# Fixed first tiles for eight experts, small last groups in a linear attention, and an order for norms and scatters

## The chip, the cores and the metric

The program runs on one NeuronCore of a Trainium2 chip, in float32 throughout. The metric is the device time of one execution in microseconds (us). Five engines work side by side, each through its own instructions in order: TensorE (PE, matmuls; PEld are its weight loads), VectorE (DVE), ScalarE (ACT), GpSimd (POOL) and SyncE (SP, which here only issues DMAs and reads registers). A DMA is issued by SP, ACT or POOL and carried out by 16 DMA engines. Engines wait for each other through semaphores.

## The reference

Two layers work on x of shape (2, 256, 56, 56). Layer 0 is a group norm, a 1x1 and a depthwise 3x3 convolution to q, k, v, and two neighbourhood attentions (7x7, dilations 1 and 2). Layer 1 turns the image into 6272 tokens of 256 channels and applies a linear attention block and then a mixture of experts:

```python
t = _to_tokens(x)
t = t + _L1_attn_ref(_ln_t(t), ...)   # elu+1 linear attention, layer norm, 512-wide MLP, layer norm
t = t + _L1_ffn_ref(_ln_t(t), ...)    # 8 experts, top 2 of a softmax
x = _from_tokens(t, x)
```

In the experts, each token goes through the two experts that its router likes best, and the results are weighted and added:

```python
h = gelu(einsum('end,edh->enh', xe, W1) + b1)      # 256 -> 1024, per expert
y = einsum('enh,ehd->end', h, W2) + b2             # 1024 -> 256
out = (weights[:, :, None] * sel).sum(axis=1)      # the two chosen experts
```

## The kernel before, in words

The tile framework (`tc`) inserts all semaphores. It also chooses the order of instructions on every engine: it plays the program through with its own clock and issues what is ready, earlier source lines first among ready ones; `tc.high_priority()` puts a block ahead of other ready work, and `tc.issue_after` holds a block behind one instruction. Only TensorE's order in the linear attention is written out by hand (`tc.manual_schedule`). The order is fixed when the program is built; the chip then runs each queue in that order.

**Front.** Convolutions and neighbourhood attention write tokens to `td` in HBM. Behind the last of these stores (`anchors["tokens"]`, L805), SP copies NDUM = 7 blocks of 256 filler rows (`c_fill`, 260 KB each) into the spare region of `xs` (L807). `check_sums` (L811) and then `layer1` (L1070) follow; `layer1` first loads the tokens of the second image, `t_b`, on SP (L1078, L197).

**Linear attention.** The 6272 tokens are 49 blocks of 128. `groups` are six groups of 4 blocks (0 to 23), block 24, and six groups of 4 (25 to 48); written (first block, number of blocks). `order` (L1414) runs them with block 24 last. A software pipeline over steps s (L1421) has five generators in flight: `queries` for order[s], `message` for order[s-1], `feed_forward` for order[s-2], `route` for order[s-3], and the rest of `route` ("p") for order[s-4]. The string in L1434 says in which sequence their parts are traced, and that is TensorE's order:

```python
for part in "mqfpufmuqfurfvrfvfv":
    next(on.get(part, iter(())), None)
```

`feed_forward` has one part for each of four 128-wide hidden blocks (matmuls `p`, L1279) and one part for each two blocks of its second matmul (`py`, L1291), after which a norm's power (POOL, L222), a scaling (DVE `u`, L1300) and an addition to `t_b` (POOL, L1304) follow. `route` starts with `stats` on that sum (DVE L214, L215, L221; POOL power L222), a second power (L1353), and the normalised row (L137), which TensorE transposes (`pts`, L1151). Its second part computes router logits (`pl`, L1371) and the top two (L1307 to L1340). Its third part ranks tokens within their experts (`pp`, L1386 and L1387), turns ranks into row numbers `si` (L1395), and POOL scatters the rows to `xs` in HBM (L143), two indirect DMAs a block. Expert e owns rows from e * RG on, in order of arrival; `cnt` counts them.

**Experts.** When `cnt` is final, a matmul and some twenty small DVE operations make tables (L1473 to L1519): how many 256-row tiles each expert has, and for each of NTL = 56 tiles its expert (`tab[:, 0]`, one-hot `oh`) and first row (`tab[:, 1]`). SP reads eight registers and copies 256 filler rows behind the last row of each expert (L1527). Then for each tile, SP reads expert and row from the table and `fetch` (L1533) loads the rows `xr`, 1 MB `w1e`, 1 MB `w2e` and the bias `b2e`; TensorE transposes (`px`, L1570), multiplies (`ph`, L1581, `py`, L1589); ACT does the gelu (L1585), POOL scatters results to `y` (L1599). At the end, `y` is read back, added and transposed out (L1603).

Of the kernel before, what the change touches and what calls it, by code (L numbers as in the profile page):

```python
# [11 lines left out]
F32 = mybir.dt.float32  # L12
AF = mybir.ActivationFunctionType
ALU = mybir.AluOpType
AX = mybir.AxisListType
# [3 lines left out]
P = 128  # L19
# [20 lines left out]
E = 8  # L40
FF = 1024
NJ = FF // P
N = B * T
K = 2
ST = 256
RG = T * B + ST
NTL = (N * K + E * (ST - 1)) // ST
NDUM = NTL - N * K // ST
XW = C + 4


def shape_constants():
# [24 lines left out]
    def key_masks(n, nk):  # L77
# [18 lines left out]
        "c_steps": np.tile(ST * np.arange(N // ST + 1, dtype=np.float32), (P, 1)),  # L96
        "c_cum": np.tile((np.arange(E)[:, None] >= np.arange(E)[None]).astype(np.float32), (P, 1, 1)),
        "c_tile": np.tile(np.arange(NTL, dtype=np.float32), (P, 1)),
# [10 lines left out]
def hybrid_kernel(ctx: ExitStack, tc: tile.TileContext, a: dict, out: bass.AP):  # L109
# [98 lines left out]
    def stats(sm, t):  # L208

        n = t.shape[1]  # L210
        st = sm.tile([P, 4, 6], F32, name="st")
        mv = sm.tile([P, 4, 2], F32, name="mv")
        for k in range(n):
            nc.vector.bn_stats(st[:, k, :], t[:, k, :])  # L214
            nc.vector.bn_aggr(mv[:, k, :], st[:, k, :])  # L215
        return mv, rstd(sm, mv[:, :n, 1], 1.0)
# [112 lines left out]
    def front(ph):  # L329
# [474 lines left out]
        with tc.issue_after(anchors["tokens"]):  # L804
            for i in range(NDUM):  # L805
                nc.sync.dma_start(xs[E * RG + i * ST : E * RG + (i + 1) * ST, :], a["c_fill"][E + i])
# [263 lines left out]
    def layer1(ctx, tk):  # L1070
# [5 lines left out]
        groups = [(4 * i, 4) for i in range(6)] + [(24, 1)] + [(25 + 4 * i, 4) for i in range(6)]  # L1076
        for n0, n in groups[7:]:
            tk.load(n0, n)  # L1078

        with ExitStack() as ph:  # L1080
# [8 lines left out]
            def load(name, src, shape):  # L1089
                w = wp.tile(shape, F32, name=name)  # L1090
                nc.gpsimd.dma_start(w, src)
                return w
# [63 lines left out]
            def parts(n0, n):  # L1156

                if n == 4:
                    return [(n0 // 25, 0, 4 * P)]
                return [(0, 0, P // 2), (1, P // 2, P)]  # L1160
# [181 lines left out]
            def route(n0, n):  # L1342
# [3 lines left out]
                mv, rs = stats(sm, t)  # L1346
                rs = rs[:, :n]
                u = sm.tile([P, 4], F32, name="u4")[:, :n]
                nc.vector.tensor_tensor(u, mv[:, :n, 1], rs, ALU.mult)
                nc.vector.tensor_tensor(u, u, rs, ALU.mult)  # L1350
                nc.vector.tensor_scalar(u, u, 1e-5, None, ALU.add)
                rs2 = sm.tile([P, 4], F32, name="rs2")[:, :n]
                nc.gpsimd.tensor_tensor(rs2, u, mhalf[:, :n], ALU.pow)  # L1353
# [60 lines left out]
            order = groups[:6] + groups[7:] + groups[6:7]  # L1414
# [4 lines left out]
            with tc.manual_schedule(engines={mybir.EngineType.PE}):  # L1419
                on = {}  # L1420
                for s in range(ng + 4):  # L1421
                    on = {"p": on.get("r", iter(()))}
                    if s < ng:
                        on["q"] = queries(*order[s], qzs)
                    if 1 <= s < ng + 1:
                        on["m"] = message(*order[s - 1], qzs.pop(0), m2Ts)
                    if 2 <= s < ng + 2:
                        on["f"] = feed_forward(*order[s - 2], m2Ts.pop(0))
                    if 3 <= s < ng + 3:
                        on["r"] = route(*order[s - 3])  # L1430
                    if s < 6:
                        for k in range(2):
                            on["uv"[k]] = keys(tk, wk, sm, ps_a, 4, kx, acc, groups[7 + s][0] + 2 * k, 2)
                    for part in "mqfpufmuqfurfvrfvfv":  # L1434
                        next(on.get(part, iter(())), None)
                    if s == 5:
                        kxs = wk.tile([P, 2, C], F32, name="kxs", tag="u")
                        kc = sm.tile([P, 2], F32, name="kc")
                        close_keys(tk, ps_a, kx, acc, kxs, kc)
                        sums[1] = merged(1, kxs, kc)  # L1440
# [3 lines left out]
        with ExitStack() as ph:  # L1444
            wp = ph.enter_context(tc.tile_pool(name="p4w", bufs=1))
            w1p = ph.enter_context(tc.tile_pool(name="p4w1", bufs=3))
            w2p = ph.enter_context(tc.tile_pool(name="p4w2", bufs=3))
# [6 lines left out]
            def load(name, src, shape):  # L1454
# [10 lines left out]
            steps = load("steps", a["c_steps"], [P, N // ST + 1])  # L1465
            cum = load("cum", a["c_cum"], [P, E, E])
            tnum = load("tnum", a["c_tile"], [P, NTL])
            enum = load("enum", a["c_e"], [P, E])
            ones = wp.tile([P, P], F32, name="ones4")
            nc.vector.memset(ones, 1.0)  # L1470


            pc = ps_t.tile([P, E], F32, name="pc", tag="pt")  # L1473
            nc.tensor.matmul(pc, ones, cnt, start=True, stop=True)
            ce = wp.tile([P, E], F32, name="ce")
            nc.vector.tensor_copy(ce, pc)

            endf = wp.tile([P, E], F32, name="endf")
            nc.vector.tensor_tensor(endf, ce, ebase, ALU.add)
            endi = wp.tile([P, E], mybir.dt.int32, name="endi")  # L1480
            nc.vector.tensor_copy(endi, endf)

            ns = N // ST + 1
            gt = wp.tile([P, E, ns], F32, name="gt")
            nc.vector.tensor_tensor(
                gt, ce.unsqueeze(2).to_broadcast([P, E, ns]),
                steps.unsqueeze(1).to_broadcast([P, E, ns]), ALU.is_gt,
            )
            nt = wp.tile([P, E], F32, name="nt")
            nc.vector.tensor_reduce(nt, gt, AX.X, ALU.add)  # L1490
            nc.vector.tensor_tensor(cum, cum, nt.unsqueeze(1).to_broadcast([P, E, E]), ALU.mult)
            incl = wp.tile([P, E], F32, name="incl")
            nc.vector.tensor_reduce(incl, cum, AX.X, ALU.add)

            ge = wp.tile([P, NTL, E], F32, name="ge")
            nc.vector.tensor_tensor(
                ge, tnum.unsqueeze(2).to_broadcast([P, NTL, E]),
                incl.unsqueeze(1).to_broadcast([P, NTL, E]), ALU.is_ge,
            )
            et = wp.tile([P, NTL], F32, name="et")  # L1500
            nc.vector.tensor_reduce(et, ge, AX.X, ALU.add)
            nc.vector.tensor_scalar(et, et, float(E - 1), None, ALU.min)
            etm = wp.tile([P, NTL], F32, name="etm")
            nc.vector.tensor_scalar(etm, et, -float(E), None, ALU.add)
            tab = wp.tile([P, 2, NTL], mybir.dt.int32, name="tab")
            nc.vector.tensor_copy(tab[:, 0, :], et)
            skip = wp.tile([P, E], F32, name="skip")
            nc.vector.tensor_scalar(skip, nt, -float(ST), float(RG), ALU.mult, ALU.add)
            nc.vector.tensor_tensor(ge, ge, skip.unsqueeze(1).to_broadcast([P, NTL, E]), ALU.mult)
            rt = wp.tile([P, NTL], F32, name=f"rt{run}")  # L1510
            nc.vector.tensor_reduce(rt, ge, AX.X, ALU.add)
            nc.vector.scalar_tensor_tensor(rt, tnum, float(ST), rt, ALU.mult, ALU.add)
            nc.vector.tensor_scalar(rt, rt, float(E * RG + (NDUM - 1) * ST), None, ALU.min)
            nc.vector.tensor_copy(tab[:, 1, :], rt)
            oh = wp.tile([P, NTL, E], F32, name="oh")
            nc.vector.tensor_tensor(
                oh, et.unsqueeze(2).to_broadcast([P, NTL, E]),
                enum.unsqueeze(1).to_broadcast([P, NTL, E]), ALU.is_equal,
            )  # L1519

# [6 lines left out]
            for e in range(E):  # L1527
                r = value(endi[0:1, e : e + 1], E * RG - ST)
                ins = nc.sync.dma_start(xs[bass.ds(r, ST), :], a["c_fill"][e])
                tc.declare_no_dep(ins.ins, group=f"xs{run}", reason="rows of their own")  # L1530
                tc.add_to_no_dep_group(f"xs{run}", ins.ins)

            def fetch(t):  # L1533
                e = value(tab[0:1, 0, t : t + 1], E - 1)
                r = value(tab[0:1, 1, t : t + 1], E * RG + (NDUM - 1) * ST)
                xr = xp.tile([P, 2, XW], F32, name="xr")
                nc.sync.dma_start(xr, xs[bass.ds(r, ST), :].rearrange("(p j) c -> p j c", j=2))
# [13 lines left out]

            for t in range(NTL):
                xr, w1e, w2e, b2e = fetch(t)

                eq = xp.tile([P, 2], F32, name="eq")
                nc.vector.tensor_scalar(eq, xr[:, :, C + 3], etm[:, t : t + 1], None, ALU.is_equal)
# [4 lines left out]
                so = xp.tile([P, 4 + NJ, E], F32, name="so")  # L1561
                nc.gpsimd.tensor_tensor(  # L1562
                    so, sel, oh[:, t, :].unsqueeze(1).to_broadcast([P, 4 + NJ, E]), ALU.mult
                )
                sv = xp.tile([P, 4 + NJ], F32, name="sv")
                nc.vector.tensor_reduce(sv, so, AX.X, ALU.add)  # L1566
# [112 lines left out]
```

## Time and profile before

| | |
|---|---|
| median of six runs | 2289.43 us (2281.72 to 2294.22) |
| profiled execution, its own time | 2296.86 us |
| span of its trace | 2295.1 us |
| busy: PE / PEld / DVE / ACT / POOL | 2047.4 / 1434.9 / 1037.4 / 630.1 / 670.2 us |
| front | 0 to about 809 us |
| linear attention, first `t_b` load to last scatter | about 820 to 1373 us |
| tables and filler rows, up to the first expert matmul | about 1373 to 1392 us |
| experts | about 1392 to 2215 us |
| read back and output | about 2216 to 2295 us |

The span is cut out of one execution by the hardware profiler; its times are microseconds from the first instruction. A line of the time-ordered view gives start, duration, engine, source line, operation, written tile and read tiles, how many were merged, and in brackets how long the engine had been idle and what ended that. A line of the table by stretches gives the length of the stretch, each engine's busy time with its number of instructions, TensorE's granted clock as a share of full speed, and what the DMA engines did.

### The profile page before, as it was taken

To read this page: it belongs to the slowest core of one execution; us is meant where nothing else is said; L and a number is where in the kernel's file an instruction comes from. 1 tells how busy PE (TensorE), PEld (TensorE's weight loads), DVE (VectorE), ACT (ScalarE), POOL (GpSimd) and SP (SyncE) were. 2 spreads that over 40 slices of the span, in tenths; PEclk is the share of its full clock that TensorE was granted. 3 is DMA by queue.
4 is the path that set the end of the run, shared out by engine and by line. 5 is a ranking of instruction groups with operands and counts; after the bars stand their busy time and mean duration, and the time that the engine had idled before them with its cause. 6 is when DMAs were issued, how large, how long until landed. Compare 5 with 4: busy or idle time off the path is not lost.

```text
span 2295.1 us, 28356 instructions
## 1 busy us (share of the span) xinstructions
PE 2047.4 (89%) x10344; PEld 1434.9 (63%) x10344; DVE 1037.4 (45%) x2499; ACT 630.1 (27%) x1253; POOL 670.2 (29%) x838
## 2 busy tenths in 40 slices
PE   6899899999988868999999937999999999999963
PEld 3444344554355545666566626888888888888852
DVE  6769867957965543565545441111111111111113
ACT  1223333233332313332333202222222222222210
POOL 5621101120033233453444551222222222222233
PEclk9999889999898979999999968999999999999975
DMA  4643313351522040000001027555555555555537
GB/s 96 155 110 106 95 56 103 97 146 39 159 65 48 26 157 1 1 29 28 26 31 38 33 61 273 187 187 191 192 192 187 187 188 187 190 191 192 170 116 236
DMA packets 175393, 273.79 MB, mean 119 GB/s; under 512 B 24246, under 2 KB 123012, under 8 KB 175006
## 3 DMA queue, kind: packets, MB, share of 16 engines
q1 hardware_dynamic: 155726, 229.99, 32.8%
q0 software_dynamic: 11680, 32.05, 4.1%
q10 hardware_dynamic: 7840, 9.86, 1.2%
q8 instruction: 84, 1.38, 0.3%
q14 instruction: 63, 0.52, 0.1%
HBM read 210.54 MB, written 65.31 MB: 120 GB/s over the span
## 4 chain that ended last, share of the span: by engine, by line
PE 65%; DVE 15%; POOL 5%; DMA 4%; ACT 3%; issue 3%; SPq 1%; DVEq 0%; POOLq 0%; ACTq 0%
PE ph L1581 17%; PE py L1589 17%; PE p L1279 5%; PE po L540 4%; PE py L475 4%; PE pc L487 4%; DVE yc L500 3%; PE s_ps L527 2%; DVE p L531 2%; PE kp L253 2%; DMA yr<-y 2%; POOL rs L222 2%; PE s_ps L325 2%; PE kx L266 2%; PE py L1291 1%
## 5 line engine op out<-in xcount | busy, mean ns | idle before, releaser
L1581 PE MATMUL ph<-xe,w1e 128*128 128x256 f32 x1792 | 401.2, 382 | 13.9 <-DVE xe L1573 10.6
L1589 PE MATMUL py<-w2e,hT 128*128 128x256 f32 x1792 | 395.9, 379 | 0.0
L1581 PEld LDWEIGHTS ph<-xe,w1e 128*128 128x128 f32 x1792 | 339.7, 191 | 66.3 <-DVE xe L1573 17.2
L1585 ACT ACTIVATE hT<-ph,sv 128x256 f32<-128x256 f32 x448 | 209.6, 474 | 598.8 <-PE ph L1581 598.2
L1589 PEld LDWEIGHTS py<-w2e,hT 128*128 128x128 f32 x1792 | 340.5, 190 | 46.3
L500 DVE SCALAR_TENSOR_TENSOR yc<-ypad,w,yc 128x1120 f32<-128x1120 f32 x192 | 267.7, 1397 | 41.2 <-ACT yc L498 38.2
L1594 DVE TENSOR_TENSOR yt<-py,b2e 128x512 f32<-128x512 f32 x56 | 38.8, 692 | 331.8 <-PE py L1589 331.8
L487 PE MATMUL pc<-ypad,diag 128*128 128x448 f32 x432 | 176.6, 549 | 0.5 <-ACT ypad L481 0.5
L531 DVE TENSOR_TENSOR p<-s_ps,tab 98x340 f32<-98x340 f32 (+5 forms) x240 | 138.1, 600 | 62.8 <-PE s_ps L527 61.0
L475 PE MATMUL py<-x_sb,wq 128*128 128x448 f32 (+1 forms) x384 | 156.3, 539 | 10.1 <-ACT yc L491 4.7
L1596 POOL TENSOR_SCALAR yt<-yt,eq 128x256 f32<-128x256 f32 x112 | 52.4, 477 | 366.5 <-DVE yt L1594 366.5
L536 ACT ACTIVATE p<-p 98x680 f32<-98x680 f32 (+5 forms) x120 | 111.8, 931 | 173.7 <-DVE p L531 168.6
L527 PE MATMUL s_ps<-qT,kT 32*98 32x170 f32 (+5 forms) x960 | 132.0, 407 | 18.7 <-DVE p L531 16.7
L1558 DVE TENSOR_TENSOR idi<-xr,eq 128x2 int32<-128x2 f32 x56 | 9.0, 161 | 288.0 <-DMA y<-yt,idi 287.9
L527 PEld LDWEIGHTS s_ps<-qT,kT 32*98 32x98 f32 (+1 forms) x960 | 58.4, 172 | 106.7 <-DVE p L531 60.0
L487 PEld LDWEIGHTS pc<-ypad,diag 128*128 128x128 f32 x432 | 78.1, 189 | 71.7 <-issue 67.6
L143 POOL DMA_INDIRECT y<-yt,idi x112 | 113.1, 1010 | 27.5 <-issue 18.4
L464 POOL TENSOR_SCALAR diag<-ident,w 128x128 f32<-128x128 f32 x108 | 84.1, 800 | 118.6 <-PE pc L487 112.0
L475 PEld LDWEIGHTS py<-x_sb,wq 128*128 128x128 f32 x384 | 70.7, 197 | 73.2 <-issue 54.7
L143 POOL DMA_INDIRECT xs<-row,si x98 | 95.9, 978 | 59.0 <-DVE si L1395 31.7
L1562 POOL TENSOR_TENSOR so<-sel,oh 128x96 f32<-128x96 f32 x56 | 21.5, 388 | 260.6 <-DVE sv L1566 257.8
L222 POOL TENSOR_TENSOR rs<-rs,mhalf 128x2 f32<-128x2 f32 (+2 forms) x88 | 64.9, 744 | 107.8 <-DVE rs L221 101.4
(280 smaller groups left out, 2719.4 us busy)
## 6 DMA issues: line engine op xcount, KB each, us to landing
w1e<-in_L_ffn_W SPq DMA_DIRECT2D x56, 1024.0 KB
w2e<-in_L_ffn_W SPq DMA_DIRECT2D x56, 1024.0 KB
yd<-yc SPq DMA_DIRECT2D x24, 784.0 KB
xr<-xs SPq DMA_DIRECT2D x56, 260.0 KB
ld<-yd SPq DMA_DIRECT2D x28, 448.0 KB
yr<-y SPq DMA_DIRECT2D x12, 1024.0 KB
b2e<-in_L_ffn_b SPq DMA_DIRECT2D x56, 128.0 KB
out<-o_sb ACTq DMA_DIRECT2D x24, 256.0 KB
```

Source lines behind the costliest of these rows:

```text
L143: ins = nc.gpsimd.indirect_dma_start(out=dst[:, :], out_offset=bass.IndirectOffsetOnAxis(ap=index, axis=0), in_=src, in_offset=None,)
L222: nc.gpsimd.tensor_tensor(r[:, :n], r[:, :n], mhalf[:, :n], ALU.pow)
L475: nc.tensor.matmul(py[:, :n, :], wq1[:, ct, oc * P : (oc + 1) * P], x_sb[:, ct, (q0 + g0) * WW : (q0 + g0 + n) * WW], start=(ct == 0), sto ...
L487: nc.tensor.matmul(pc, diag[:, tap, :], ypad[:, dy : dy + 8, dx : dx + WW], start=(tap == 0), stop=(tap == 8),)
L500: nc.vector.scalar_tensor_tensor(yc[:, 8:, :], src, w, yc[:, 8:, :], ALU.mult, ALU.add)
L527: nc.tensor.matmul(s_ps[:nk, j, :n].rearrange("p (i j) -> p i j", j=nj), kT[hs], q[hs], start=True, stop=True,)
L531: nc.vector.tensor_tensor(p[:nk, 2 * pr : 2 * pr + 2, :n].rearrange("p h (i j) -> p h i j", j=nj), s_ps[:nk, :, :n].rearrange("p h (i j) - ...
L536: nc.scalar.activation(p[:nk, :, :n], p[:nk, :, :n], AF.Exp)
L1279: nc.tensor.matmul(p1[:, :w], fw1[:, k, oc * P : (oc + 1) * P], rhs, start=(k == 0), stop=(k == 3))
L1581: nc.tensor.matmul(p1, w1e[:, ct, j * P : (j + 1) * P], xe[:, ct, :], start=(ct == 0), stop=(ct == 1),)
L1585: nc.scalar.activation(hT[:, j, :], p1, AF.Gelu, bias=sv[:, 4 + j : 5 + j])
L1589: nc.tensor.matmul(py[:, h, :], hT[:, j, h * P : (h + 1) * P], w2e[:, j, :], start=(j == 0), stop=(j == NJ - 1),)
```

## The change

1. **Order and size of the last groups.** The last group of four (45, 4) becomes (45, 2) and (47, 2), and block 24 comes before them. The list is now defined ahead of its use and has 14 entries instead of 13, and steps with no new queries use another string.
2. **Route's norms.** `stats`, the second power and what lies between them get high priority.
3. **First tiles.** Tile e < 8 is always expert e's first 256 rows: expert, row and bias selection are known when the program is built. Rows of `xs` that this tile may read but nobody writes are filled by eight more copies beside the seven in the front. The tables (now for 48 tiles) and the eight copies of filler rows, now starting no earlier than row 256 of an expert, are traced after tiles 0 and 1; the first eight `xr` loads and those copies are declared to be independent of each other.
4. **Weights' memory.** The pools of constants, `w1e` and `w2e` wait for the old tiles that they overlap instead of for whole old pools.

```diff
+            for e in range(E):
+                nc.sync.dma_start(xs[e * RG : e * RG + ST, :], a["c_fill"][e])
             for i in range(NDUM):
...
+        order = groups[:6] + groups[7:12] + [(24, 1), (45, 2), (47, 2)]
...
-                if n == 4:
-                    return [(n0 // 25, 0, 4 * P)]
+                if n > 1:
+                    return [(n0 // 25, 0, n * P)]
...
-                mv, rs = stats(sm, t)
...
-                nc.gpsimd.tensor_tensor(rs2, u, mhalf[:, :n], ALU.pow)
+                with tc.high_priority():
+                    mv, rs = stats(sm, t)
...
+                    nc.gpsimd.tensor_tensor(rs2, u, mhalf[:, :n], ALU.pow)
...
-            order = groups[:6] + groups[7:] + groups[6:7]
...
-                    for part in "mqfpufmuqfurfvrfvfv":
+                    for part in "mqfpufmuqfurfvrfvfv" if s < ng else "mfpffmfrfrff":
...
-            w1p = ph.enter_context(tc.tile_pool(name="p4w1", bufs=3))
+            w1p = ph.enter_context(tc.tile_pool(name="p4w1", bufs=3, reuse_waits="tile"))
...
+            def make_tables():
...
+                nc.vector.tensor_scalar(endf, ce, float(ST), None, ALU.max)
+                nc.vector.tensor_tensor(endf, endf, ebase, ALU.add)
...
+                    for group in (f"xs{run}", f"first{run}"):
+                        tc.declare_no_dep(ins.ins, group=group, reason="rows of their own")
+                    tc.add_to_no_dep_group(f"fill{run}", ins.ins)
...
             def fetch(t):
-                e = value(tab[0:1, 0, t : t + 1], E - 1)
-                r = value(tab[0:1, 1, t : t + 1], E * RG + (NDUM - 1) * ST)
                 xr = xp.tile([P, 2, XW], F32, name="xr")
+                if t < E:
+                    e, r = t, t * RG
+                else:
+                    e = value(tables.tab[0:1, 0, t - E : t - E + 1], E - 1)
+                    r = value(tables.tab[0:1, 1, t - E : t - E + 1], E * RG + (NDUM - 1) * ST)
+                rows = xs[t * RG : t * RG + ST, :] if t < E else xs[bass.ds(r, ST), :]
+                ins = nc.sync.dma_start(xr, rows.rearrange("(p j) c -> p j c", j=2))
+                if t < E:
+                    tc.declare_no_dep(ins.ins, group=f"fill{run}", reason="rows of their own")
+                    tc.add_to_no_dep_group(f"first{run}", ins.ins)
...
             for t in range(NTL):
+                if t == 2:
+                    make_tables()
                 xr, w1e, w2e, b2e = fetch(t)
...
+                if t < E:
+                    sv = sel[:, :, t]
+                else:
```

## The prediction

> **What bounds the kernel now.** I read the busy times by stretch first. TensorE is nearly full up to 1325 us and from 1400 us on; between them lies the hole that most of the change is about:
>
> ```profile
> 1300.00:1325.00 25.00, 25.00 (x106) 16.43 (x104) 11.70 (x60) 6.33 (x19) 13.36 (x16) 1.00 0.12 43
> 1325.00:1350.00 25.00, 7.16 (x48) 7.00 (x48) 7.34 (x30) 1.96 (x6) 13.23 (x14) 0.66 0.12 44
> 1350.00:1375.00 25.00, 6.74 (x28) 5.31 (x27) 15.67 (x92) 1.18 (x5) 12.53 (x16) 0.61 0.25 70
> 1375.00:1400.00 25.00, 9.26 (x31) 7.60 (x32) 3.61 (x17) 3.99 (x7) 2.10 (x6) 0.57 0.79 260
> ```
>
> The first busy column is TensorE's; the 0.66, 0.61, 0.57 are its granted clock. Next, the time-ordered view of that hole, first its entry:
>
> ```profile
> 1331.29 1.06 POOL L143 DMA_INDIRECT xs<-row,si  x1 [0.81 <-DVE st L214]
> 1331.51 0.17 DVE L221 TENSOR_SCALAR rs<-mv 128x4 f32<-128x4 f32 x1
> ...
> 1341.24 1.05 POOL L222 TENSOR_TENSOR rs<-rs,mhalf 128x4 f32<-128x4 f32 x1
> 1342.97 1.01 POOL L1353 TENSOR_TENSOR rs<-u,mhalf 128x4 f32<-128x4 f32 x1 [0.68 <-DVE u L1351]
> 1344.97 1.94 PE L1151 MATMUL pts<-ident,row 128*128 128x128 f32 x8 [17.84 <-DVE row L137]
> ```
>
> The variance of (45,4) is ready at 1331.68, but its power stands behind eight scatters of (41,4), 9.95 us. Then the exit:
>
> ```profile
> 1371.63 0.96 POOL L143 DMA_INDIRECT xs<-row,si  x1 [0.30 <-DMA xs<-row,si]
> 1372.89 8.60 SPq L1529 DMA_DIRECT2D xs<-in_c_fill  x8
> 1384.55 0.40 SPq L1537 DMA_DIRECT2D xr<-xs  x1
> 1385.53 0.39 SPq L1539 DMA_DIRECT2D w1e<-in_L_ffn_W  x1
> 1387.45 1.09 PE L1570 MATMUL px<-ident,xr 128*128 128x128 f32 x4 [20.40 <-DMA xr<-xs]
> 1387.65 0.35 SPq L1537 DMA_DIRECT2D xr<-xs  x1
> 1391.83 9.43 PE L1581 MATMUL ph<-xe,w1e 128*128 128x256 f32 x32 [3.29 <-DMA w1e<-in_L_ffn_W]
> 1398.09 0.23 DVE L1556 TENSOR_SCALAR eq<-xr,etm 128x2 f32<-128x2 f32 x1 [8.52 <-DMA xr<-xs]
> ```
>
> After the last scatter (ends 1372.59) come eight filler copies, their landing, rows, weights, and only then `ph`. The last line shows a DMA queued behind others: the second `xr`, issued at 1387.65 behind 2 MB of weights, landed 10.4 us later, 4.5 us per MB. Last, the place where the front is touched:
>
> ```profile
> 809.76 5.15 SPq L806 DMA_DIRECT2D xs<-in_c_fill  x7
> 820.05 7.83 SPq L197 DMA_DIRECT2D t_b<-td  x6
> 827.73 0.75 DVE L214 BATCH_NORM_STATS2 st<-t_b 128x6 f32<-128x256 f32 x2 [3.26 <-DMA t_b<-td]
> ```
>
> The first `t_b` is on the chain that ended last (7.59 us of it), so what delays it delays the stage.
>
> **Term 1, the tail: the last scatter.** I follow TensorE's strings from step 11, which starts at 1230.5 in both. Full-clock prices for a group of 4: pm 3.5, pq 3.45, each hidden block 3.45, py 7.0, pl 1.7, pts and mts 0.9, pp 0.7, pd 1.75; for 2, half.
> - Step 11 now has q(24,1): its twin before lasted 33.65 (1265.03 to 1298.68). Step 12 is the old step 13 (25.1) plus q(45,2), 2.6: step 13 starts at 1291.9.
> - Step 13 has only 8.2 us of matmuls before pts(41,4). Before, py to the normalised row took 12.0 (1265.03 to 1277.03); with priority I take 10.9, plus one scatter that slips in, 1.3. pts at 1304, step 14 at 1309.7.
> - Step 14 is 14.3 us of matmuls, to 1324.0. The eight scatters of (41,4) run from about 1317 to 1328, and they still hold the power of py(45,2), which has no priority, for about 4.
> - Step 15: pp(24,1) waits for its top two (3.7: 1361.1 to 1364.8); pts(45,2) at 1335.7, py(47,2) ends 1339.8, pl(45,2) 1340.7.
> - Steps 16 and 17, one chain: py to pts of (47,2) 9, to 1349; transposes, evacuation and pl 2.5; top two 4.7 to 4.9 (1291.78 to 1296.43); pp 0.7; row numbers 1.6 (1357.65 to 1359.25); four scatters of 1.27 end at 1363.6, 9 earlier than before's 1372.59; landing 1.8 (1289.37 to 1291.15), 1365.4.
>
> Splitting adds waits on the way, so 9 is less than the 10 that the priority alone would give; bounds from -2 (none of the priority arrives) to 17 (no wait but the chain).
>
> The Trainium skill, page "TensorE: Matmul & The Clock Gate", section "Part 1: The HAM clock gate", speaks against small groups: an idle window of about 3.4 us halves the clock until another busy one. Four new waits at half of 3.4 us would be 7 us by it, an estimate. The rows have this price already: cold pts 1.94 against 0.87, cold pl 1.98 against 1.70; I go by them, some 2 us, inside the above.
>
> **Term 2, the exit.** Removed from before `ph`: eight register reads and copies (1372.89 to 1381.49), their landing, and two table reads. What remains: `xr` issued at 1365.5, landing 2.9 (1384.55 to 1387.45), px 1.1, `xe` 1.0 (1388.58 to 1389.57): `ph` at about 1371 instead of 1391.83. Terms 1 and 2 together: 21 earlier. This needs `w1e` to be there. Its slots lie on the old stage's weights and `xT_b`, last read by py and pl, around 1340 to 1351, and on `tri`, `ones`, `ebase`, last read around 1357. SP's order goes by readiness (chk_r, L818, stands before the older store L764 at 808.87 against 809.33), so I place them ahead of `xr`. If they stay behind, `w1e` lands 1365.5 + 1 + 6.2 = 1372.7: +2.
>
> But what is ahead is also in front of `xr` in the ring. If 3 MB go at 1351 and a fourth at 1357, 14 us at 4.5 us per MB have moved 3.1 MB when `xr` is issued, and 1 MB is left: 0 to 4.5, I take +2.
>
> The tables move off the path: the 22 small DVE operations (1366.11 to 1376.3) now fall under POOL's scatters or tile 0's matmuls (16 us); the eight copies have 30 us until tile 2. If that cover went, see the second rival. Tiles 0 to 7 lose one POOL (0.39) and one DVE operation (0.25) and two register reads each, all under 14.5 us of matmuls: 0. More loads on ACT's queue (0.5 each) are the old ones earlier: 0, ACT is idle 19 us there. An extra step costs nothing else on TensorE, whose total is the same.
>
> **Term 3, the front.** Eight more copies of 260 KB stand on SP ahead of `t_b`. Issue: 15 at 0.735 end at 820.8, 0.75 behind the old 820.05. Transfer: 2.1 MB at the 332 to 367 GB/s that this stretch moves is 6.2. Cover: DVE's work behind `st` (means and masks, 1.1 + 1.1 us and more) can be planned ahead of it, and `t_b`'s transposes (838.5) come only after mwp. Bounds 0 and +12; I take +4. POOL's own loads share the DMA engines with SP's queue either way, since `t_b` followed at once.
>
> The skill's page "DMA: Bandwidth & Descriptors", section "Queues, rings and completion order", has engines take turns between queues packet by packet. While POOL's weights are loading, SP would get half, and 2.1 MB cost 12 us, an estimate, if they lasted so long; at the total rate the trace gives 6.
>
> **Term 4, priority in the full steps.** TensorE bounds them (34.5 a step, 33.7 by the prices above). Row statistics come first on DVE, elu and z slide by up to 1 us under hidden blocks of 3.45: 0, bounds -3 and +3.
>
> Sum: -21 + 2 + 4 + 0 = -15 us. The profiled execution took 2296.86 (span 2295.1, 1.8 around it), 7.4 above the median; the sum goes onto the median: 2289.4 - 15 = 2274.
>
> **Rivals.**
> - *POOL's order does not change* (the change doesn't do what it says): the scheduler's clock may find scatters ready before the powers, as at 1331.29. Then each of the last routes waits for the scatters ahead: 8 + 8 + 4 of them, 25 us less some 5 counted. The last scatter ends at about 1384, `ph` at 1391: -21 + 20 + 2 + 4 = +5, 2294. It decides from 15 us on. For it: the row at 1341.24. Against: exactly these powers get priority, and most scatters take 10 of 34 us.
> - *The tables become the wait*: TensorE's tiny matmul for `cnt` planned behind tile 1 (about 1403) holds SP's register reads, then come 1.6 of DVE, 8.6 of copies, and `w1e` 6.2 of tile 2: ready at 1420, 17 late. -15 + 17 = +2, 2291. Against: before, such matmuls went when ready (1366.48).
> - *The ring is full*: all six weight slots and eight copies, 8.1 MB, from 1351 at 4.5 per MB last until 1387. `xr` lands then, `ph` at 1389: 2289 - 3 + 4 = 2290. Half of it: 2282.
> - *The front is free and the tail clean*: without terms 3 and the 2 us, 2268; with two waits fewer in the tail 2262.
>
> **How the numbers follow.** Forecast 0.50 (own range 2268 to 2281), clean 0.17, ring half or whole 0.13, tables 0.07, POOL's order 0.13. No change can be told within about 0.3%, 7 us: faster means under 2282.5. Faster: forecast and clean less 0.04, in which the front's +12 meets a fuller ring, and half of the ring's chance less 0.03 for the same reason: 0.67. Same: tables, the ring's other half and half of POOL's order: 0.20. Slower: the other half of POOL's order and those 0.07: 0.13. The range from 2262 to 2291 leaves out 0.2.
>
> **What would show it.** The power of the second `t_b` sum ahead of scatters on POOL; last scatter ending near 1364 plus the front's delay; `xr` within 1 us of its landing, filler copies not between; `w1e` issued earlier than `xr`; first `ph` about 17 us earlier than 1391.83, and everything from there unchanged; `t_b` landing at 832 to 834. Wrong would be: last scatter after 1380, `xr` more than 6 us in flight, TensorE idle before tile 2, or a stage between 830 and 1230 whose length changes by over 5 us.

## The result and the profile after

The changed kernel is slower: median 2298.75 us (2293.78 to 2311.39) against 2289.24 us for the kernel before on the same chip; ratio 1.0049, 95% interval 1.0038 to 1.0060, by which the change costs about 11 us (the two medians differ by 9.5), where 15 less were forecast. Its profiled execution took 2303.97 us, span 2302.1.

What lies ahead of layer 1 is the same code in both, but takes 798 to 811 us in the executions seen here. So I cut each trace at events of its own and count from the issue of the first weight load of layer 1 (`w_v` on POOL; 809.39 before, 804.92 after). "py" is the start of the first `py`, "steps" from there to the sixth `pp`, "tail" on to the end of the last scatter, "exit" on to the first `ph`, "experts" to the end of the span. All in us, worked out from the time-ordered view of one profiled execution of each kernel; the ratio is of all its runs:

| kernel | py | steps | tail | exit | experts | ratio to before (95%) |
|---|---|---|---|---|---|---|
| before | 101.5 | 260.6 | 201.1 | 19.2 | 903.3 | |
| changed | 110.6 | 264.1 | 211.0 | 6.3 | 905.3 | 1.0049 (1.0038 to 1.0060) |
| difference | +9.1 | +3.5 | +9.9 | -12.9 | +2.0 | sum +11.6 |
| forecast | +4 | 0 | -9 | -10 | 0 | sum -15 |

"Experts" spreads from 902.0 to 907.6 over the runs below, nearly all of which have the changed kernel's code there; I read nothing into its +2.0.

Busy times by stretch of the changed kernel (length; busy us and instructions of PE, PEld, DVE, ACT, POOL; granted clock of TensorE; DMA share; GB/s):

```profile
1300.00:1325.00 25.00, 21.34 (x113) 18.56 (x112) 12.29 (x55) 6.54 (x22) 14.41 (x15) 0.86 0.12 44
1325.00:1350.00 25.00, 15.97 (x71) 13.09 (x70) 10.31 (x57) 6.29 (x21) 12.87 (x18) 0.92 0.12 44
1350.00:1375.00 25.00, 13.80 (x58) 11.98 (x58) 11.04 (x70) 2.92 (x9) 7.93 (x12) 0.70 0.15 53
1375.00:1400.00 25.00, 9.09 (x31) 7.13 (x31) 8.09 (x52) 1.54 (x3) 7.95 (x9) 0.50 0.57 167
```

The hole did not close. It is spread over more and smaller waits: the first stretch, full before, now has 3.7 us of idle TensorE.

Some lines of the tail of the changed kernel in order of time (start, duration, engine, line, operation, in brackets the idle time before it and what ended it; line numbers are those of the changed file, and other lines stand between them):

```profile
1319.71 1.92 PE L1377 MATMUL pl<-wr,xT_b 128*128 128x8 f32 x16
1325.30 0.19 DVE L1318 TENSOR_TENSOR prob<-pl,sd 128x32 f32<-128x32 f32 x1 [5.40 <-PE pm L1254]
...
1330.76 0.41 PE L1392 MATMUL pp<-chosen,tri 128*128 128x32 f32 x2 [3.84 <-DVE chosen L1384]
...
1344.74 0.96 POOL L144 DMA_INDIRECT xs<-row,si  x1 [0.30 <-DMA xs<-row,si]
1347.42 0.18 POOL L1368 COPY row<-dest 128x2 f32<-128x2 f32 x1 [1.72 <-remote]
1347.57 0.73 POOL L223 TENSOR_TENSOR rs<-rs,mhalf 128x2 f32<-128x2 f32 x1
1348.33 0.88 DVE L1305 SCALAR_TENSOR_TENSOR u<-py,rs,g 128x256 f32<-128x256 f32 x2 [3.82 <-POOL rs L223]
1353.90 0.59 PE L1392 MATMUL pp<-chosen,tri 128*128 128x8 f32 x2 [8.86 <-DVE chosen L1384]
1362.78 3.62 PE L1296 MATMUL py<-fw,hTl 128*128 128x256 f32 x16
...
1389.59 0.96 POOL L144 DMA_INDIRECT xs<-row,si  x1 [0.30 <-DMA xs<-row,si]
```

The power at 1347.57 is that of py(45, 2), which has no priority. Ahead of it in POOL's queue stand eight scatters and then a small copy, `row<-dest`, which idles 1.72 us. The view calls what ended this only "remote"; by the program, the copy writes into one of two row buffers, and the eight scatters read that one, so it is their landing. DVE's next instruction, `u`, waits 3.82 us for the power; the top two of the one-row group stand behind `u` on DVE; `pp` of that group waits 8.86 us for them on TensorE; and py(47, 2) stands behind `pp`. The exit is as forecast:

```profile
1366.43 16.23 SPq L1561 DMA_DIRECT2D w1e<-in_L_ffn_W  x2
1392.13 0.35 SPq L1556 DMA_DIRECT2D xr<-xs  x1
1395.10 1.08 PE L1599 MATMUL px<-ident,xr 128*128 128x128 f32 x4 [10.97 <-DMA xr<-xs]
1396.82 8.94 PE L1610 MATMUL ph<-xe,w1e 128*128 128x256 f32 x32 [0.64 <-DVE xe L1602]
```

Two `w1e` go ahead of `xr` (the first line holds both, issued at 1366.43 and 1382.29), `xr` lands 3.0 us after its issue, and `ph` starts 6.3 us after the last scatter instead of 19.2. Last, the front; `hb` are 16 small matmuls that make a bias out of `g1b` and `fw`:

```profile
805.29 5.84 SPq L807 DMA_DIRECT2D xs<-in_c_fill  x8
811.17 6.88 SPq L809 DMA_DIRECT2D xs<-in_c_fill  x7
818.53 11.92 SPq L198 DMA_DIRECT2D t_b<-td  x6
823.93 0.71 POOL L1118 DMA_DIRECT2D g1b<-in_L_attn_g  x1 [8.13 <-DMA fw<-in_L_attn_W]
828.01 1.22 DVE L1128 TENSOR_REDUCE wmean<-fw 128x4 f32<-128x1024 f32 x1 [7.25 <-DMA fw<-in_L_attn_W]
828.28 0.73 POOL L1118 DMA_DIRECT2D g1b<-in_L_attn_b  x1 [3.64 <-DMA fw<-in_L_attn_W]
833.81 3.54 PE L1137 MATMUL hb<-g1b,fw 128*128 128x1 f32 x16 [1.16 <-DMA g1b<-in_L_attn_b]
857.30 3.43 PE L267 MATMUL kx<-xt,ks 128*128 128x256 f32 x8 [2.08 <-DVE ks L207]
```

Before:

```profile
824.10 0.71 POOL L1113 DMA_DIRECT2D g1b<-in_L_attn_g  x1 [3.75 <-DMA fw<-in_L_attn_W]
825.99 0.73 POOL L1113 DMA_DIRECT2D g1b<-in_L_attn_b  x1 [1.18 <-DMA fw<-in_L_attn_W]
832.86 3.41 PE L1132 MATMUL hb<-g1b,fw 128*128 128x1 f32 x16
```

POOL's two waits on `fw` were 3.75 and 1.18 us and are 8.13 and 3.64, and DVE now waits 7.25 for `fw` where it waited 3.26 for `t_b`. It is not `t_b` that comes too late first but the weights `fw`, which POOL's own queue loads at the same time, and through them `hb`: 28.9 us after `w_v`'s issue instead of 23.5.

### The profile page after: what moved, and what is told of

Same layout as the page of the kernel before. It is cut to its first block, busy times and chain, and to the rows that moved or that the text cites. A ratio compares the mean times of both kernels' runs of the same rounds, so it can differ in the third digit from the quotient of the medians.

```text
span 2302.1 us, 28421 instructions
## 1 busy us (share of the span) xinstructions
PE 2052.1 (89%) x10392; PEld 1446.9 (63%) x10392; DVE 1039.0 (45%) x2542; ACT 631.5 (27%) x1264; POOL 667.8 (29%) x834
## 5 line engine op out<-in xcount | busy, mean ns | idle before, releaser
L1614 ACT ACTIVATE hT<-ph,sv 128x256 f32<-128x256 f32 x384 | 179.3, 473 | 519.8 <-PE ph L1610 519.4
L1284 PE MATMUL p<-m2T,fw 128*128 128x512 f32 (+2 forms) x224 | 95.6, 551 | 0.0
```

The costliest lines, as they stand in the source:

```text
L1284: nc.tensor.matmul(p1[:, :w], fw1[:, k, oc * P : (oc + 1) * P], rhs, start=(k == 0), stop=(k == 3))
L1614: nc.scalar.activation(hT[:, j, :], p1, AF.Gelu, bias=sv[:, 4 + j : 5 + j])
```

## The experiments

Each run was timed against the kernel before on its own chip. The table goes on with the columns of above. The stretches of a row and its ratio differ by up to 6 us, since the first are of one execution. Kernels that differ only in the fills of the front differ in the tail by some 2 us (e4 and e5, e8 and e9), so a difference of the tail below that shows nothing.

| run | py | steps | tail | exit | experts | ratio to before (95%) |
|---|---|---|---|---|---|---|
| e1 fills late | 103.9 | 264.2 | 208.4 | 6.1 | 907.0 | 0.9999 (0.9982 to 1.0016) |
| e2 old order | 110.5 | 264.1 | 198.4 | 6.4 | 904.7 | 0.9984 (0.9969 to 0.9999) |
| e3 no priority | 110.4 | 260.5 | 210.8 | 6.2 | 905.5 | 1.0011 (0.9995 to 1.0027) |
| e4 exit alone | 101.4 | 260.5 | 202.8 | 6.4 | 904.7 | 0.9963 (0.9948 to 0.9978) |
| e5 all fills late | 101.4 | 260.6 | 200.8 | 6.3 | 903.9 | 0.9933 (0.9909 to 0.9957) |
| e6 other string | 110.3 | 264.0 | 218.5 | 6.2 | 902.0 | 1.0064 (1.0041 to 1.0088) |
| e7 unsplit | 107.6 | 264.2 | 208.0 | 6.2 | 904.0 | 1.0016 (1.0000 to 1.0032) |
| e8 tail priority | 104.2 | 260.5 | 194.9 | 6.3 | 902.9 | 0.9927 (0.9903 to 0.9952) |
| e9 e5 and e8 | 97.8 | 260.5 | 196.8 | 6.3 | 904.3 | 0.9933 (0.9908 to 0.9957) |
| e10 fills alone | 109.3 | 260.5 | 201.7 | 16.8 | 904.0 | 1.0033 (1.0016 to 1.0051) |
| e11 split, one row last | 109.2 | 264.1 | 204.1 | 6.4 | 907.1 | 1.0032 (1.0012 to 1.0051) |
| e12 one row early | 108.9 | 251.4 | 221.3 | 6.2 | 904.3 | 1.0053 (1.0034 to 1.0071) |
| e13 copy on ACT | 108.5 | 302.5 | 227.8 | 10.1 | 904.2 | 1.0286 (1.0266 to 1.0305) |
| e14 e9, copy on ACT | 101.1 | 295.1 | 233.6 | 6.4 | 904.2 | 1.0228 (1.0207 to 1.0248) |
| e15 copy behind | 108.1 | 263.7 | 204.7 | 6.1 | 902.8 | 1.0007 (0.9990 to 1.0024) |
| e16 e9, copy behind | 98.3 | 260.3 | 196.5 | 6.5 | 902.8 | 0.9916 (0.9893 to 0.9939) |
| e17 e7, copy behind | 108.2 | 263.9 | 206.3 | 6.1 | 907.6 | 1.0019 (1.0004 to 1.0035) |
| e18 mended | 100.4 | 260.3 | 208.2 | 6.3 | 905.9 | 0.9975 (0.9957 to 0.9994) |

**One part undone at a time, and the exit alone.**

```diff
 e1: the eight fills not in the front, but
+        for n0, n in groups[7:]:
+            last = tk.load(n0, n)
+        with tc.issue_after(last.ins):
+            for e in range(E):
+                nc.sync.dma_start(xs[e * RG : e * RG + ST, :], a["c_fill"][e])
 e2:
-        order = groups[:6] + groups[7:12] + [(24, 1), (45, 2), (47, 2)]
+        order = groups[:6] + groups[7:] + groups[6:7]
-   "mqfpufmuqfurfvrfvfv" if s < ng else "mfpffmfrfrff"
+   "mqfpufmuqfurfvrfvfv"
 e3:
-                with tc.high_priority():
 e4: e1, e2 and e3 together
```

> The changed kernel, with its eight extra fills issued behind the six loads of t_b instead of ahead of them. Theory (the fills at the front hold up the loads that the stage starts with, 9.1 us by the first py against the start of the fills: 910.86 - 809.76 = 101.1 before, 915.50 - 805.29 = 110.2 after): 9 us less than the changed kernel, about 2290, and the first py 101 us behind the first fill again. Rival (the 9 us come from the planned order of DVE or the weights, the fills only happen to stand there): no difference, about 2299.

> The changed kernel with the old order of the groups and the old TensorE string; fills, high priority and the fixed first tiles stay. Theory (the small groups and the string cost the time in the tail: POOL's queue with scatters and row copies, then DVE and TensorE in their orders behind it): the last scatter, 1390.55 in the changed kernel, falls to between 1370 (priority then saves the 10 us of scatters ahead of the last power) and 1381 (it saves nothing), so 10 to 20 us less, 2279 to 2289. Rival (the priority or the prefetched weights hold up the tail, whatever the order): 2296 to 2300.

> The changed kernel without the high priority of route's statistics and powers. Theory (priority costs 3.5 us in steps 2 to 6, py at 953.29 to 1085.14 before and 958.72 to 1093.24 after, and helps the tail by less than it should): the growth of the shift between 950 and 1090 goes, -3.5; in the tail the powers of (45,2) and (47,2) stand behind the scatters again, +0 to +10: 2295 to 2305. Rival (the priority is what pushes the row copy and the scatters ahead of py's power): the tail gets shorter by 10 or more, 2282 to 2286.

> The kernel before, with only the fixed first tiles and the tables behind them (the exit), the extra fills behind t_b; old order, old string, no priority. Theory (the exit alone saves 13 us, 19.2 to 6.3 from the end of the last scatter to the first ph, and late fills cost nothing): 2276 to 2279, 0.5% faster than before. Rival (the extra 2 us of the experts' stage and the fills' transfer, wherever they are, eat a good part): 2283 to 2288.

Fills: py falls by 6.7 with priority (e1, where 9 were expected) and to before's 101.4 without (e4), and the times follow; the fills hold up the front. Order: it costs 12.6 of tail (211.0 to 198.4), inside the theory's 10 to 20. Priority: it costs 3.6 in the full steps in every pair (264.1 against 260.5) and does nothing in the tail of the new order (211.0, 210.8), where e3's theory had a loss without it, but saves 4.4 in that of the old (202.8 to 198.4). By its ratio e3 gains some 9 us on the changed kernel, by its stretches 4; no run explains the rest. The exit alone is faster than before by 0.2 to 0.5%.

**The fills by themselves, and all fifteen moved.**

```diff
 e5: e4, and behind the eight fills
+            for i in range(NDUM):
+                nc.sync.dma_start(xs[E * RG + i * ST : E * RG + (i + 1) * ST, :], a["c_fill"][E + i])
 e10: the kernel before, and ahead of its seven fills
+            for e in range(E):
+                nc.sync.dma_start(xs[e * RG : e * RG + ST, :], a["c_fill"][e])
```

> The version with the exit alone (e4) with the seven fills that the kernel before had at the front put behind t_b as well, so that all fifteen follow it. Theory (a fill ahead of t_b costs 9.1 / 8 = 1.1 us each, since fills and the weights on the other queue share the transfer): the first py comes about 8 us earlier from the first weight load, 93.5 instead of 101.4, 2271. Rival (seven of them lie under the linear attention's own matmuls and cost nothing; only what goes beyond them did): 101 again, 2279.

> The kernel before with nothing but the eight extra fills ahead of t_b added (they are written and not used). Theory (the fills alone hold up fw and g1b, and through them TensorE's hb, by 5 us, and the longer idle time costs clock): hb at 28.5 instead of 23.5 from the first weight load, the first py at 108 to 111, the tail and all else as before: +6 to +9 us, ratio 1.003 to 1.004. Rival (what held up hb was the changed kernel's plan): hb at 23.5, ratio 1.000.

e10 settles it: nothing but eight copies ahead, and `hb` goes from 23.5 to 28.2, py from 101.5 to 109.3. In e5 `hb` starts at 20.6, 2.9 earlier than before, but py is at 101.4 again; e9 with the same fills has `hb` at 19.5 and py at 97.8. So 5.4 of the 9.1 us lie ahead of `hb` (23.5 to 28.9) and 3.7 behind it. Some 2 of these are the clock. The interval from the first `pd` to the first `pm` (both matmuls of `message`) is 12.3 to 12.6 in the kernel before, e4, e7, e9, e13, e16 and e17, and 13.8 to 14.3 in the others. In it stands the same group of eight `kx` matmuls (the sums of the keys), which took 1.99 us before and 3.43 after. Their line before, and the stretch from 854 to 858 with its granted clock, were

```profile
854.14 1.99 PE L266 MATMUL kx<-xt,ks 128*128 128x256 f32 x8 [2.08 <-DVE ks L206]
854.00:858.00 4.00, 3.86 (x18) 3.42 (x19) 0.08 (x1) 0.10 (x1) 1.27 (x1) 1.00 0.00 0
```

and the stretch with most of the same matmuls in the changed kernel

```profile
858.00:862.00 4.00, 4.00 (x13) 3.24 (x12) 0.00 (x0) 0.00 (x0) 0.66 (x1) 0.61 0.00 0
```

The wait ahead of them is the same 2.08 us in both, so its length alone does not decide whether the clock drops. The Trainium skill, page "TensorE: Matmul & The Clock Gate", section "Part 1: The HAM clock gate", states that the window in which activity is watched runs freely, and that the number of slow matmuls at a kernel's start therefore varies from run to run. That would fit; with one trace of each kernel, no run here shows whether the plan or the single execution decides. The size is shown: among the kernels with all fills early, `hb` to py takes 79.7 in e7, e13 and e17 and 81.0 to 82.2 in the others. The last 1.7 of the 9.1 (79.7 against 78.0 before) no run explains.

**The tail: TensorE's string, the split, the place of the one-row group.**

```diff
 e6, the changed kernel with
-   "mqfpufmuqfurfvrfvfv" if s < ng else "mfpffmfrfrff"
+   "mqfpufmuqfurfvrfvfv" if s < ng else "mfffmffprr"
 e7, with the old string and
+        order = groups[:6] + groups[7:12] + [(24, 1)] + groups[12:]
 e11, with the old string and
+        order = groups[:6] + groups[7:12] + [(45, 2), (47, 2), (24, 1)]
 e12, with the old string and
+        order = groups
```

> The changed kernel with another TensorE order in the last steps: the ranks' matmuls (pp) of the route before stand behind all hidden blocks and py, not behind the first hidden block. Theory (in the changed kernel py(47,2) is late because TensorE's order has three hidden blocks and the row's transposes behind pp(24,1), which waits 8.86 us, and because py(45,2)'s power stands behind eight scatters that pp(41,4) released): from the last full pp to the last scatter's end 211 falls by 8 to 15, the run to about 2285 to 2291. Rival (DVE's own order and work carry the chain and TensorE only follows): a fall of at most 3, 2296 to 2299.

> The changed kernel with the group of one row still ahead of the last group, but that last group whole (45,4) and the old string. Theory (it is the split that costs, since each of two small groups goes through py, power, row, top two and ranks with nothing to fill TensorE): the stretch from the sixth pp to the last scatter, 211.0 in the changed kernel and 198.4 with the old order, comes to between 198 and 204, 2284 to 2290. Rival (moving the one-row group ahead is what costs, it delays everything behind it and the split then wins some back): 208 to 215, 2296 to 2303.

> The changed kernel with the last group split into (45,2) and (47,2), but the group of one row behind them as in the kernel before, and the old string. Theory (in the tail, moving the one-row group ahead costs 9.6, the split 3.0, by e2, e7 and the changed kernel): from the sixth pp to the last scatter's end 198.4 + 3 = 201, 2285 to 2290. Rival (split is bad only together with the move, or it is the small groups that do harm in any place): 198 or less, or 206 to 211.

> The changed kernel with the one-row group still earlier, as the seventh step, where TensorE is full, the last group whole and the old string. Theory (TensorE's 8.6 us of work for the one row lay under the last chain's wait of 13 to 18 us before, and any place ahead of that puts it on the path): from the first py to the last scatter's end 472, as with e7 (264.2 + 208.0), where e2 has 462.5. Rival (what costs is the place next to the last group, where its steps have little work beside their waits): 463 to 466.

e6 is slower in the tail by 7.5, where 8 to 15 less were expected. Its TensorE and POOL in order of time:

```profile
1333.61 0.30 PE L1392 MATMUL pp<-chosen,tri 128*128 128x32 f32 x2
1335.81 1.05 POOL L144 DMA_INDIRECT xs<-row,si  x1 [10.57 <-DVE rs L222]
1336.89 1.26 POOL L223 TENSOR_TENSOR rs<-rs,mhalf 128x1 f32<-128x1 f32 x2
1344.42 0.66 PE L1156 MATMUL pts<-ident,row 128*128 128x128 f32 x2 [10.28 <-DVE row L138]
```

POOL's order, planned when the program is built, has the first scatter of (41, 4) ahead of the power of the one-row group. I had made that scatter late by moving `pp` behind py; POOL stood idle for 10.57 us with the power behind the scatter, and TensorE's transposes waited. e7 goes to its rival's lower edge (208.0): putting the one-row group ahead costs 9.6 against e2, with no split at all. e12 shows that it is not the place next to the last group. With that group at the seventh step, far from the end, py to the last scatter takes 251.4 + 221.3 = 472.7 (472 expected; e2 462.5): its feed-forward and route, which ran in and behind the last chain's wait, cost about 10 in both places ahead of it. The wait itself stays, 17.84 before, 12.39 in e7 (18.31 in e12), now with nothing beside it. e11 (204.1) lies between its two forecasts. It differs from e2 by the split alone, which costs 5.7 there; with the one-row group ahead, split and string together cost 3.0 (e7 to the changed kernel).

**The row copy.**

```diff
 e13 (changed kernel) and e14 (e9)
-                nc.gpsimd.tensor_copy(row[:, :n, C], dest[:, n0 : n0 + n])
+                nc.scalar.copy(row[:, :n, C], dest[:, n0 : n0 + n])
 e15 (changed kernel), e16 (e9, below), e17 (e7)
+                    power = nc.gpsimd.tensor_tensor(rs2, u, mhalf[:, :n], ALU.pow)
+                with tc.issue_after(power.ins):
+                    nc.gpsimd.tensor_copy(row[:, :n, C], dest[:, n0 : n0 + n])
```

> The changed kernel with the copy of dest into the row moved from POOL to ACT, so that no instruction in POOL's queue waits for the landing of earlier scatters ahead of py's power. Theory (the copy, not only the scatters, holds up the power of py(45,2): DVE's u idles 3.82 us there, 1.72 of it the copy's wait for the landing): the power follows the last scatter at once, 1.7 to 4 us less from the sixth pp to the last scatter's end, 207 to 209 instead of 211. Rival (the scatters alone hold it, or DVE's next instruction is late anyway): 210 to 212.

> The best version so far (e9) with the same copy on ACT. Theory: there the copy follows the last power (in e8 it stands at 1343.80, behind the row's normalisation), so it costs nothing: tail 195 to 197, ratio 0.992 to 0.993 as e9. Rival (the copies' waits also hold up powers in the full steps): steps 258 to 259 instead of 260.5, ratio 0.991 or less.

> The changed kernel with the copy of dest into the row still on POOL, but fixed behind the second power of its own route, so that in the queue no copy that waits for landings stands ahead of py's power. The order of everything else on POOL in the tail is the same. Theory (in the changed kernel the copy's wait of 1.72 us holds py(45,2)'s power and what follows): tail 207 to 209.5 instead of 211.0. Rival (the eight scatters alone hold it): 210 to 212.

> e7 (one-row group ahead of the whole last group, old string) with the copy of dest fixed behind the second power as in e15. Theory (what the place costs is TensorE's work taken out from under the last chain's wait; the copies have no part in it): from the sixth pp to the last scatter 207 to 208.5 as in e7 (208.0), 9 to 10 above the old order's 198.4. Rival (the copies' waits make up a part there too, as the 6.3 us of e15): 202 to 205.

By the ratios e13 is 54 us slower than the changed kernel and e14 67 us slower than e9, which neither theory had; the full steps alone lose 38 and 35. On ACT in one of e13's:

```profile
1109.53 0.20 ACT L1368 COPY row<-dest 128x4 f32<-128x4 f32 x1 [9.65 <-DMA xs<-row,si]
1109.63 0.68 ACT L1287 ACTIVATE hTl<-p,hb_sb 128x512 f32<-128x512 f32 x1
```

A copy of 0.2 us waits 9.65 us for the landing of the earlier scatters, and on ACT the hidden activations that TensorE waits for stand behind it. So the wait is real, but these two runs do not tell what it costs on POOL. e15 does. There, on TensorE, DVE and POOL in order of time,

```profile
1316.47 1.85 PE L1378 MATMUL pl<-wr,xT_b 128*128 128x8 f32 x16
1318.36 0.19 DVE L1318 TENSOR_TENSOR prob<-pl,sd 128x32 f32<-128x32 f32 x1 [2.07 <-PE pl L1378]
1323.88 0.41 PE L1393 MATMUL pp<-chosen,tri 128*128 128x32 f32 x2 [0.28 <-DVE chosen L1385]
1337.86 0.96 POOL L144 DMA_INDIRECT xs<-row,si  x1 [0.30 <-issue]
1338.83 0.75 POOL L223 TENSOR_TENSOR rs<-rs,mhalf 128x2 f32<-128x2 f32 x1
```

the power follows the last scatter at once, and the tail is 6.3 shorter, more than the 1.5 to 4 expected. Only part of it is the copy. The first three lines show another wait gone: `prob` starts 0.04 us after `pl`'s end here, and 3.67 after it in the changed kernel. e18 below has the copy behind and the late `prob` (3.26), and a tail of 208.2: that gives some 2.8 to the copy (211.0 to 208.2) and 3.5 to `prob` (208.2 to 204.7), an estimate, as e18 differs from the other two in fills and priority as well. e17's tail (206.3, between its two forecasts) is 1.7 shorter than e7's, where `prob` is late too (1.31 behind `pl`; 0.03 in e17); the place of the one-row group still costs 7.9 against e2, somewhat under the theory's 9 to 10.

**Versions that beat both.**

```diff
 e8: e4 with
+                with tc.high_priority() if n0 >= 37 or n == 1 else ExitStack():
 e9: e5 and e8
 e16: e9 with the copy behind the powers, as in e15
 e18: the changed kernel with e5's fills, e8's priority and e15's copy; its own order, groups and string
```

> The version with the exit alone (e4: old order, late extra fills) with high priority in the last four routes only. Theory (priority costs 3.6 us in the full steps and 0 to 2 at the front and saves 4.4 in the tail, 202.8 to 198.4 by e4 and e2, the two independent): steps 260.5 as in e4, tail 198.4, 4.4 us less than e4, 2275. Rival (what the priority saves in the tail needs the state that the earlier priorities left in the plan): tail 202 to 203, 2279.

> Old order, exit, all fifteen fills behind t_b, priority in the last four routes only (e5 and e8 together). If the stretches add up: py at 101 (e5), steps 260.6, tail 195 to 198 (e8, e2), exit 6.3: 7 us less than e4 by the stretches, ratio 0.992 to 0.993. If the 3 us that e5 wins at the start of TensorE's work (hb at 20.6 instead of 23.3) are not lost again to a slower granted clock: 98 to 99, 0.991.

> The best version (e9) with the same copy behind the powers. Theory (in the old order the copies of the last groups follow the last powers anyway, and in the full steps TensorE hides them): stretches as e9 within 2 us, ratio 0.992 to 0.994. Rival (the copies' waits cost the full steps something): steps 258 to 259 instead of 260.5.

> The changed kernel's own order, small groups and string, mended in the three places that the runs name: all fifteen fills behind t_b, priority in the last routes only, the copy behind the powers. If the parts add up: py at 98, steps 260.4, tail 204.7 or a little less, exit 6.3: 575 to the first ph's start less 6 to 8 against before by the stretches, ratio 0.994 to 0.996, some 8 us behind e16, which differs by the old order alone. Rival (with the waits gone the small groups win what they were made for): tail 196 or less, as fast as e16.

e8 has both halves of its theory: the steps stay at 260.5 and the tail falls by 7.9, more than the 4.4. In it one wait of the kernel before answers:

```profile
1339.32 1.94 PE L1157 MATMUL pts<-ident,row 128*128 128x128 f32 x8 [13.35 <-DVE row L138]
```

17.84 before, 4.5 less: the two powers now go between the scatters of (41, 4), not behind the last. e8 and e9 are not to be told apart, nor e9 from e16, whose stretches agree within 0.5 in the linear attention (the intervals of the two ratios overlap). e16 is the fastest, 0.6 to 1.1% faster than before (2267.65 us). e18 is 0.1 to 0.4% faster than before. Its tail (208.2, where 204.7 was expected) is 11.7 longer than e16's, which differs from it by the old order, groups and string: with the rest mended, the new ones still lose.

## Why the prediction was wrong

**Term 2, the exit: right.** Issue to landing of `xr` 3.0 (2.9 forecast), `px` 1.1, `xe` 1.0, `w1e` ahead of `xr`, tables hidden; 12.9 saved, where the forecast's own times (1371 - 1363.6 against 19.2) make 11.8. The +2 for the ring's backlog was not there: only two `w1e` (2 MB) went ahead, at 1366.43 and 1382.29, the later one 9.8 us before `xr`, and the other weights stood behind it.

**Term 1, the tail: wrong in sign** (-9 forecast, bounds -2 to 17 earlier, +9.9 measured). From run to run, the +9.9 are +1.7 for the exit (before to e4, no more than such tails differ by), -4.4 for the priority (e4 to e2), +9.6 for the place of the one-row group (e2 to e7) and +3.0 for split and string (e7 to the changed kernel). Three steps of the term failed.
- "An extra step costs nothing else on TensorE, whose total is the same." The total is the same, but its place is not: the one-row group ran in and behind the last chain's wait for the row, for nothing, and ahead of that wait costs 8 to 10 (e7, e12, e17). That is the largest single term, and the wait stood in the prediction's own lines, 17.84 us.
- "The eight scatters of (41,4) [...] still hold the power of py(45,2) [...] for about 4". The wait was priced on POOL and not followed on: `u` on DVE, the top two behind `u`, `pp` behind them, py(47, 2) behind `pp` (3.82 us became 8.86). The row copy that waits for landings, in POOL's queue ahead of the power, was not in the forecast (some 2.8 by e15 and e18); nor was the late `prob` (some 3.5). Both are parts of the sum above, not additions to it.
- "the 10 that the priority alone would give": 4.4 (e4 to e2) to 7.9 (e4 to e8) in the old order, since powers slip in among the scatters rather than pass them all, and nothing in the new order (e3).

**Term 3, the front: mechanism half right, size wrong** (+4, bounds 0 to +12; +9.1). The transfer was priced, its victim was not: the term followed `t_b`, while `fw` and `g1b` on POOL's queue, which share the DMA engines, were waited for 4 to 7 us later (19.0 and 23.4 us after `w_v`'s issue, 14.7 and 16.6 before). "POOL's own loads share the DMA engines with SP's queue either way" was the step that failed. 1.5 MB of `fw` took from its issue at 811.65 to 825.99 before, 14.3 us, and from 807.18 to 828.28 after, 21.1. The rule that was weighed there, engines taking turns between queues (the Trainium skill, "DMA: Bandwidth & Descriptors", "Queues, rings and completion order"), gave 12 for `t_b`, and the total rate 6.2; `hb` came 5.4 later (4.7 in e10), nearer to the second, but the rows do not show whose packets went first. Of the other 3.7 us some 2 are TensorE's clock, for which the term had nothing, and 1.7 are open.

**Term 4, priority in the full steps: wrong** (0, bounds -3 to +3; +3.5). e3 and e4 take it away to 0.1. The loss comes at 1.1 to 1.3 us a step up to the third `pp` and then stops. "TensorE bounds them" overlooked that steps up to the fifth have DVE work for keys as well: `kx` in one of them waits 1.45 us for DVE's `ks`, 0.82 before (0.89 in e3).

**The rivals.** None is what happened. "POOL's order does not change" had its sum near the truth by accident (2294): POOL's order did change, route's powers stand ahead of the scatters; it was py's power and the copy that did not. Tables and ring did nothing. Of the signs named beforehand, "last scatter after 1380" came true (1390.55), and so did a stage between 830 and 1230 longer by over 5 us; the first `ph` was 5 us later, not 17 earlier.

## What to carry to other kernels

Work that fills a wait is free only where it stands: before moving it, name the wait that covered it and what fills that wait afterwards. In queues that run in a fixed order, follow a wait through every queue behind it, and look for tiny instructions that wait for something slow: a 0.2 us copy behind a DMA's landing, once in every step, cost 54 and 67 us on one engine and by an estimate some 3 on another. A transfer that is moved ahead delays not only what follows on its own queue, but the loads that other queues run at that time.

## What the runs showed of the hardware

- DVE's first instruction on the router logits (`prob`) starts 0.03 to 0.05 us after `pl`'s end in nearly all groups; with scatters under way on POOL or just over, it came 3.67 (changed kernel), 3.52 (e13), 3.50 (e6), 3.34 (e3) and 3.26 us (e18) late, in these five 1.3 to 1.6 us after the burst's last scatter, and 2.09 (e1), 1.31 (e7) and 1.10 us (e8) late in three more; elsewhere up to 0.9, in the kernel before 0.66. In e15, e11 and e9 it started within such a burst without delay. The view names TensorE's `pm` or `py` as what ended the wait in the changed kernel, e3, e18 and e1, and "remote" in e6 and e13; in e18 `prob` starts 0.3 us before `pm` ends and 1.4 after `py`. What holds it stays open, and no run here tests it.
- The same eight `kx` matmuls took 1.99 us (before) or 3.43 us (changed kernel) at the same wait of 2.08 ahead of them, with granted clocks of 1.00 and 0.61 over 4 us.
- A stretch ahead of everything that was edited ended between 798 and 811 us in single profiles; the steps inside the linear attention repeat to some tenths (260.3 to 260.6 in the nine kernels without priority there and with the copy on POOL), the tail only to some 2 us.
